# A two-layer RWKV stack with an FP4 feed-forward: where the recurrence keeps its scaled factors, how GpSimd's sums are cut, and what the planner reckons between engines

## The chip, the core and the metric

The kernel runs on one core of one Trainium2 chip. The metric is the device time of one execution in microseconds (us). Before the change the median of three runs is 3125.28 us (3124.25 to 3128.61). All of the arithmetic is float32.

The engines are named as the profile names them: PE (TensorE; PEld is its loading of weights), DVE (VectorE), ACT (ScalarE), POOL (GpSimd) and SP (SyncE, which here only issues DMAs).

## What is computed

The input `x` has 2 batches of 4096 rows of 256 channels. A conditioning vector gives six rows per batch (`sa, ca, ga, sb, cb, gb`). Cut to what matters, the reference is:

```python
h = layernorm(x) * (1 + ca) + sa
for i in range(2):                          # two RWKV layers
    h = h + time_mix(ln(h) * ln1_w[i])
    h = h + channel_mix(ln(h) * ln2_w[i])
x = x + ga * (ln(h) * ln_out_w)
h = layernorm(x) * (1 + cb) + sb
return x + gb * fp4_ffn(h)                  # gate, up, silu, down; inputs and weights rounded to FP4

# time_mix: sx = shift(x) - x; five inputs x + sx * (maa + mix), where mix comes of a small
# tanh projection; from them r = sigmoid(.. Wr), k = .. Wk, v = .. Wv, g = silu(.. Wg),
# w = exp(-exp(time_decay + tanh(.. td_w1) @ td_w2)); then, for each head of 64 channels:
def step(state, rt, kt, vt, wt):
    kv = kt[:, None] * vt[None, :]
    out = rt @ (state + u[:, None] * kv)
    return state * wt[:, None] + kv, out
# the outputs are normalised by head, times gn_w plus gn_b, times g, times Wo
# channel_mix: sigmoid(.. cWr) * (square(relu(.. cWk)) @ cWv)
```

## The kernel before

**Tiles and streams.** A tile is 256 rows of one batch (`TT`), so each batch has 16 tiles, and each tile passes two layers and the feed-forward. There are 64 passes of `time_mix`, of `channel_mix` and of the recurrence, and 64 feed-forward chunks of 128 rows. The work is written as generators, called streams: `first_layer` and `second_layer` for each batch, `ffn_inputs`, two `ffn_chunks`, `ffn_weights` and `conditioning`. A pass alone has long waits for one engine by another. Several streams run side by side so that one fills the waits of the others.

**The planner.** No order of instructions is written by hand. `Plan.record` takes each operation into a queue of its stream, with a reckoned duration (`weight`). `Plan.run` then gives the operations out one by one: of those that could start soonest it takes the one with the least lateness and age (`min(can)`). When an operation may start is reckoned in `Plan.after`: the end of its producer plus `LAT` of the producer's engine plus `SEEN` of the consumer's (55 ns for PE, 80 for POOL, 35 for others), or plus `SAME` if both are on one engine. A change of the form of PE's tiles is charged `TURN` (94 ns), and leaving ACT's table 1283 ns. The whole plan is drawn `PLANS` = 8 times with different random ages (`JITTER`), and the drawing whose reckoned end is earliest is built. Each engine then executes its own list in order; semaphores hold an instruction until its operands are there. The planner's numbers thus set only the order.

**Buffers.** Work lives in a stock of 36 equal buffers (`SLOTS`, called `slot` in the profile), 4 double ones for r and k of the recurrence (`SLOTS2`, `slot2_n` in the code, `slot` in the profile), 5 `long` ones for the feed-forward, and 5 PSUM banks (`bank`). A stream is only read further while at least `LEAST` buffers are free.

**The recurrence, `wkv`.** It is computed in chunks of 128 rows, without a step for each row. For levels l = 0 to 6, blocks of 2^l rows meet their neighbours: `products(l)` forms the scores between the two halves of each pair of blocks, and then one DVE operation multiplies half of the elements of r and k in place by the decay of the neighbouring block (the half that `pair_view` picks: r in the later half of each pair, k in the earlier). The products of level l need the factors after the updates 0 to l-1. Level 0 uses copies of r and k with the bonus u in them (`r0`, `k0`, two slots). In the code before, the products are issued at these steps of the loop:

```python
for m in {0: (), 1: (0, 1)}.get(l, (l,)):
    products(m)
```

so levels 0 and 1 come together and each later level alone. Scores of levels 0 to 3 and of levels 4 to 6 lie in the same PSUM columns (`pa`). They are copied from there at l = 3 (by DVE under a mask, into `diag`) and at l = 6 (level 4 by DVE, 5 and 6 by ACT into `attn`). Then follow transposes of k, the state's products and the output's. The whole is under `head_lock`: one pass at a time.

**PE's forms.** Most matmuls use the array whole, 128 rows by 128 columns. The products of levels 0 to 5 use pieces of 64 rows by 32 columns (32 matmuls for each level 0 to 4, 16 for level 5), level 6 pieces of 64 by 64 (8), and the small projections pieces of 32 by 128, 64 by 128 and 128 by 64. The profile writes the form ahead of the shape (`64*32`), and counts each float32 matmul twice.

**The five inputs, `to_input`.** For each of the two channel blocks j, a DVE operation forms (mix + maa) * sx for 256 rows out of a PSUM bank; then one POOL operation adds x to both blocks (128 x 512). There are 5 in each of 64 passes, thus 320.

Every recorded operation stands in one line of the profile, L294 (line 294, where `give_out` calls it), so groups are told apart by the names of tiles and by shape. The functions that the diff touches follow.

Of the kernel before, what the change touches and what calls it, by code (L numbers as in the profile page):

```python
# [10 lines left out]
F32 = mybir.dt.float32  # L11
# [3 lines left out]
ALU = mybir.AluOpType  # L15
# [3 lines left out]
P = 128  # L19
D = 256  # L20
J = D // P
TT = 256
# [15 lines left out]
TURNS = 30.0  # L38
SLOTS = 36
STAGGER = (12, 60)  # L40
PLANS, JITTER = 8, 8.0
SLOTS2 = 4
TINY = 16
LONG = 5
AHEAD_OPS = 24
# [72 lines left out]
class Plan:  # L118
# [10 lines left out]

    LAT = {"tensor": 170.0, "vector": 0.0, "scalar": 0.0, "gpsimd": 0.0, "sync": 2600.0, "load": 0.0}  # L130


    LAP = {"vector": 84.0, "scalar": 100.0, "gpsimd": 40.0}
    SEEN = {"tensor": 55.0, "gpsimd": 80.0}
    SAME = {"vector": 34.0, "scalar": 25.0, "gpsimd": 80.0}

# [323 lines left out]
def rwkv_adaln_fp4_kernel(ctx: ExitStack, tc: tile.TileContext, a: dict, out: bass.AP):  # L460
# [77 lines left out]
    def take_slot():  # L538
        return pl.take(stock)
# [4 lines left out]
    def give(*ts):  # L544
        stock.extend(ts)
# [7 lines left out]
    def v4(t):  # L553
        return t[:, : J * TT].rearrange("p (c j t) -> p c j t", c=C, j=J)
# [113 lines left out]
    for i in range(L):  # L668
        for b in range(B):
            nc.gpsimd.memset(state[i][b], 0.0)  # L670
            for m in range(2):
                nc.gpsimd.memset(carry[i][b][m], 0.0)
    diag = keep.tile([P, 2, C, J, 32], F32, name="diag")
    attn = keep.tile([P, 2, C, J, P], F32, name="attn")
# [83 lines left out]
    def shifted(h, ln_w, car):  # L758

        xn_s = take_slot()  # L760
        xn = v3(xn_s)
        yield from layernorm(h, xn)
        bk, pt = to_channels(xn)
        x_s = take_slot()
        xT = x_s.rearrange("p (j t) -> p j t", j=J)
        pl.vector.tensor_copy(xT[:, :, 0:1], car)
        for j in range(J):
            pl.scalar.activation(xT[:, j, 1:], pt[:, j, :], AF.Copy, scale=ln_w[:, j : j + 1])
        pl.close(bk)
        give(xn_s)  # L770
        pl.vector.tensor_copy(car, xT[:, :, TT : TT + 1])
        sx_s = take_slot()
        sx = v3(sx_s)
        pl.gpsimd.tensor_tensor(sx, xT[:, :, 0:TT], xT[:, :, 1:], ALU.subtract)
        yield
        return xT[:, :, 1:], sx, x_s, sx_s

    def lerp(x, sx, maa):
        m_s = take_slot()
        m = v3(m_s)  # L780
        for j in range(J):
            pl.vector.scalar_tensor_tensor(
                m[:, j, :], sx[:, j, :], maa[:, j : j + 1], x[:, j, :], ALU.mult, ALU.add
            )
        return m, m_s
# [18 lines left out]

    def pair_view(rk, h, n):

        v = rk[:, h : h + 1]
        return bass.AP(v.tensor, v.offset, [v.ap[0], [J * TT - h, 2], [2 * h, n], [1, h]])

# [27 lines left out]
    def wkv(i, b, rk_s, dec_s, v_s):  # L837

        S = state[i][b]
        rk = rk_s[:, : 2 * J * TT]  # L840
        r, k = (rk[:, m * J * TT : (m + 1) * J * TT].rearrange(
            "p (c j t) -> p c j t", c=C, j=J) for m in range(2))
        dec, v = v4(dec_s), v3(v_s)
        yield from take(head_lock, (i, b))
        late = pl.cur.late
        pl.cur.late = late - RUSH
        r0_s, k0_s = take_slot(), take_slot()
        r0, k0 = v4(r0_s), v4(k0_s)
        with_bonus(r0, r, 0, lay[i]["time_first"])
# [6 lines left out]
        tots_s = take_slot()  # L856
        at = 0
        def products(l):
            R, K = (r0, k0) if l == 0 else (r, k)
            wid = 64 if l == 6 else 32  # L860
            pv = pa[:, :, level_cols(l)].rearrange("p a (c j t) -> p a c j t", c=C, j=J)

            if l < NLEV:
                at0 = [(q, q) for q in (0, 32, 64, 96)]
            else:
                at0 = [(0, 32), (64, 96)] if l == 5 else [(0, 64)]
            for c in range(C):
                for j in range(J):
                    for s0, t0 in at0:
                        for p in range(2):  # L870
                            hp = slice(p * HS, (p + 1) * HS)
                            mm(
                                pv[s0 : s0 + wid, p, c, j, :], K[hp, c, j, s0 : s0 + wid],
                                queries(R[hp, c, j, t0 : t0 + wid], l), True, True,
                            )

        for l in range(7):
            h = 1 << l

            for m in {0: (), 1: (0, 1)}.get(l, (l,)):  # L880
                products(m)
            if l == 1:
                give(r0_s, k0_s)

# [3 lines left out]
            tv = tot.rearrange("p (n two) -> p n two", two=2)  # L888
            upd = pair_view(rk, h, n)
            pl.vector.tensor_tensor(  # L890
                upd, upd, tv.rearrange("p n m -> p m n").unsqueeze(3).to_broadcast([P, 2, n, h]), ALU.mult
            )
# [21 lines left out]
            yield  # L914
        give(dec_s)
        tot = tot.rearrange("p (c j) -> p c j", c=C)
        for q in range(4):
# [60 lines left out]
    def time_mix(i, b, h):  # L978
# [7 lines left out]
        for k in range(J):  # L986
            mm(pm[:, TT : 2 * TT], w["w1"][:, k, P:], xx[:, k, :], k == 0, k == J - 1)
        give(xx_s)
        mix_s = take_slot()
        mixa, mixb = mix_s[:, :TT], mix_s[:, TT : 2 * TT]  # L990
# [3 lines left out]

        def to_input(o, maa):

            m_s = take_slot()
            m = v3(m_s)
            for j in range(J):
                pl.vector.scalar_tensor_tensor(  # L1000
                    m[:, j, :], o[j], maa[:, j : j + 1], sx[:, j, :], ALU.add, ALU.mult
                )
            pl.gpsimd.tensor_tensor(m, m, x, ALU.add)
            return m_s

        def branch_pair(f, g, maa_f, maa_g):

            bks, os = zip(*(pl.bank() for _ in range(2)))
            for j in range(J):
                for e, o in zip((f, g), os):  # L1010
                    mm(
                        o[:, j * TT : (j + 1) * TT], w["w2"][e][:, j * P : (j + 1) * P],
                        mixa[E * e : E * (e + 1), :], True, True,
                    )
            ms = []
            for bk, o, maa in zip(bks, os, (maa_f, maa_g)):
                ms.append(to_input([o[:, j * TT : (j + 1) * TT] for j in range(J)], maa))
                pl.close(bk)
            return ms
# [11 lines left out]
        bk, pg = proj(w["Wg"], v3(xg_s))  # L1031
        give(xg_s)
        g_s = take_slot()
        g_t = v3(g_s)
# [6 lines left out]
        for k in range(J):  # L1041
            for c in range(C):
# [3 lines left out]
                )  # L1046
        give(xw_s)
        td_s = take_slot()
        td = td_s[:, :P]
        pl.scalar.activation(td, pd[:, :P], AF.Tanh)  # L1050
        pl.close(bk)
        yield
        xk_s, xv_s = branch_pair(1, 2, w["k_maa"], w["v_maa"])
        give(mix_s, x_s, sx_s)
        rk_s = take_slot2()
# [31 lines left out]
        if not w["centred"]:  # L1087
# [8 lines left out]
            )  # L1096
        v_s = take_slot()
        xv = v3(xv_s)
        bk, o = proj_tok(w["Wv"], [xv[:, k, :] for k in range(J)])
        pl.scalar.copy(v3(v_s), o)  # L1100
        pl.close(bk)
        give(xv_s)
        yield

        o_s = yield from wkv(i, b, rk_s, dec_s, v_s)
        bk, pt = to_channels(v3(o_s))
        give(o_s)
        oT_s = take_slot()
        oT = v3(oT_s)
# [15 lines left out]
    def channel_mix(i, b, h):  # L1125
        w = lay[i]
        x, sx, x_s, sx_s = yield from shifted(h, w["ln2_w"], carry[i][b][1])
        xk, xk_s = lerp(x, sx, w["ck_maa"])
        xr, xr_s = lerp(x, sx, w["cr_maa"])
        give(x_s, sx_s)  # L1130
        yield
        kks = []
        for g in range(FD // P // 2):
            bk, o = pl.bank()
            o = halves(o)
            for m in range(2):
                n0 = (2 * g + m) * P
                for k in range(J):
                    mm(o[:, m, :], w["cWk"][:, k, n0 : n0 + P], xk[:, k, :], k == 0, k == J - 1)
            kks.append(take_slot())  # L1140
            kg = v3(kks[-1])
            pl.scalar.activation(kg, o, AF.Relu)
            pl.close(bk)
            pl.scalar.activation(kg, kg, AF.Square)
            yield
        give(xk_s)
        sr_s = take_slot()
        sr = v3(sr_s)
        bk, o = proj_tok(w["cWr"], [xr[:, k, :] for k in range(J)])
        pl.scalar.activation(sr, o, AF.Sigmoid)  # L1150
        pl.close(bk)
        give(xr_s)
        yield
# [152 lines left out]
    def ffn_inputs():  # L1306
# [3 lines left out]
        for n in range(B * NT):  # L1310
# [5 lines left out]
            xn = v3(xn_s)  # L1316
            yield from layernorm_rows(x1, xn, rows["cb"][b], lambda c: rows["sb"][b])
            p_s = pl.take(long)
            yield from fp4(pl, xn_s, C * D, P, scales[0], p_s)
            long.append(p_s)  # L1320
            xq_s = take_slot()
            xqT = v3(xq_s)
            bk, pt = to_channels(xn)
            pl.scalar.copy(xqT, pt)
            pl.close(bk)
            give(xn_s)
            left = []
# [14 lines left out]
    def ffn_chunk(c, b, t, x1_s, xq_s, left):  # L1342
        HF = FI // 2
        cs_ = slice(c * P, (c + 1) * P)
        x1, xqT = v3(x1_s), v3(xq_s)
        hb_s = pl.take(long)
        hb = hb_s[:, :FI]
        for s in range(2):
# [12 lines left out]
            pl.close(bk)  # L1361
            yield
        p_s = pl.take(long)
        yield from fp4(pl, hb_s, FI, P, scales[1 + c], p_s)
        long.append(p_s)
        hT_s = pl.take(long)
        hT = hT_s.rearrange("p (f n) -> p f n", f=NF)
        for g in range(2):
# [8 lines left out]
            yield  # L1377
        long.append(hb_s)
        bk, y = pl.bank()
# [90 lines left out]
```

## Time and profile before

| | |
|---|---|
| median of three runs | 3125.28 us |
| the profiled execution | 3123.61 us |
| its span, first to last instruction | 3121.7 us |
| mean granted PE clock | 0.981 |
| instructions | 89,338 |
| PE's records: matmuls of form 64*32 into `pa` | 22,528 |
| ACT's loads of a table | 127, 1283 ns each |
| POOL's sums of two slots, 128 x 512, and 128 x 256 | 384 and 64 |

The span is the time between the first and the last instruction; 1.9 us of the profiled execution lie outside it. A group's line gives its busy time, the mean duration of one instruction in ns, and after the bar the idle time of the engine ahead of it, with what ended that idle time. Busy time of PE is not time at its full speed, since a matmul that starts late, or follows another form, still counts as busy from its start to a modelled end. The step from one start to the next is the better measure there.

### The profile page before, as it was taken

How to read it: one execution, taken by the hardware profiler on the slowest of the kernel's cores; microseconds unless marked ns; L12 is line 12 of the kernel's file. 1: busy time of each engine (PE TensorE's matmuls, PEld its weight loads, DVE VectorE, ACT ScalarE, POOL GpSimd, SP SyncE). 2: the span in 40 equal slices, each digit the busy share in tenths (PEclk: the TensorE clock that was granted, in tenths of full speed). 3: DMA queues.
4: the chain of work that ended last, by engine and by line, in shares of the span. 5: the costliest groups of instructions: out<-in, count | busy, mean ns of one | idle time of the engine just before them, and what ended most of it. 6: DMA issues, size and time to landing. Idle time of an engine off the chain costs nothing. (4 is left out here: it accounts for less than half of the span.)

```text
span 3121.7 us, 89338 instructions
## 1 busy us (share of the span) xinstructions
PE 2984.9 (96%) x38460; PEld 2412.9 (77%) x38460; DVE 2365.4 (76%) x6146; ACT 1615.4 (52%) x3362; POOL 940.6 (30%) x888
## 2 busy tenths in 40 slices
PE   6899999999999999999999999999999999999997
PEld 4777778778787777877778787787878778787775
DVE  6785778777877777778777787777777778766877
ACT  3565555545555556455454655546445455455442
POOL 2233323223233332332323233232332323331220
PEclk9899999999999999999999999999999999999989
DMA  4000000000000000000000000000000000000000
GB/s 141 20 14 5 10 7 15 7 15 7 9 12 7 16 8 11 11 6 17 5 11 11 5 18 5 14 8 9 13 6 17 5 8 15 9 9 9 8 13 11
DMA packets 35725, 42.53 MB, mean 14 GB/s; under 512 B 2817, under 2 KB 33537, under 8 KB 35329
## 3 DMA queue, kind: packets, MB, share of 16 engines
q1 hardware_dynamic: 35328, 36.81, 3.7%
q8 instruction: 302, 4.95, 0.7%
q14 instruction: 95, 0.77, 0.1%
HBM read 28.41 MB, written 8.39 MB: 12 GB/s over the span
## 5 line engine op out<-in xcount | busy, mean ns | idle before, releaser
L294 POOL TENSOR_TENSOR slot<-slot,slot 128x512 f32<-128x512 f32 (+1 forms) x448 | 508.9, 1152 | 961.5 <-DVE slot L294 682.0
L294 ACT ACTIVATE slot<-bank 128x512 f32<-128x512 f32 (+2 forms) x644 | 331.6, 519 | 682.8 <-PE bank L294 661.1
L294 POOL TENSOR_TENSOR tiny<-tiny,nhalf 128x2 f32<-128x2 f32 (+1 forms) x288 | 289.3, 1009 | 869.6 <-DVE tiny L294 789.4
L294 DVE TENSOR_TENSOR slot<-slot,slot 128x512 f32<-128x512 f32 x512 | 372.1, 728 | 110.2 <-PE pa L294 79.6
L294 PE MATMUL bank<-slot,small 32*128 32x256 f32 (+3 forms) x2816 | 393.3, 361 | 8.9 <-DVE slot L294 4.4
L294 PE MATMUL bank<-slot,cWk 128*128 128x256 f32 x1536 | 367.9, 385 | 2.5 <-DVE slot L294 2.0
L294 PE MATMUL bank<-cWv,slot 128*128 128x256 f32 x1536 | 343.8, 380 | 0.0
L294 PEld LDWEIGHTS pa<-slot 64*32 64x32 f32 x19456 | 224.0, 109 | 154.2 <-DVE diag L294 54.2
L294 PEld LDWEIGHTS bank<-slot,small 32*128 32x128 f32 (+3 forms) x2816 | 272.3, 178 | 88.3 <-issue 33.8
L294 PEld LDWEIGHTS bank<-slot,cWk 128*128 128x128 f32 x1536 | 284.5, 191 | 46.9 <-DVE slot L294 4.3
L294 PEld LDWEIGHTS bank<-cWv,slot 128*128 128x128 f32 x1536 | 289.2, 190 | 39.8 <-issue 0.3
L294 PE MATMUL pa<-slot 64*32 64x16 f32 x19456 | 266.2, 191 | 43.0 <-DVE diag L294 23.7
L294 ACT ACTIVATE slot<-bank,small 128x256 f32<-128x256 f32 (+1 forms) x640 | 248.4, 449 | 111.6 <-PE bank L294 109.9
L294 DVE SCALAR_TENSOR_TENSOR slot<-bank,small,slot 128x256 f32<-128x256 f32 x640 | 271.8, 473 | 24.9 <-PE bank L294 23.9
L294 DVE TENSOR_TENSOR slot<-slot,bank 128x512 f32<-128x512 f32 x192 | 131.0, 682 | 189.3 <-PE bank L294 143.0
L294 POOL TENSOR_TENSOR slot<-slot 128x512 f32<-128x512 f32 x128 | 141.9, 1111 | 346.8 <-ACT slot L294 272.3
L294 ACT ACTIVATE slot<-slot 128x512 f32<-128x512 f32 x288 | 181.3, 633 | 42.8 <-DVE slot L294 38.0
L294 DVE TENSOR_TENSOR long<-long,bank 128x352 f32<-128x352 f32 x256 | 131.1, 514 | 93.0 <-ACT long L294 69.8
L294 DVE SCALAR_TENSOR_TENSOR slot<-slot,small,slot 128x256 f32<-128x256 f32 x384 | 186.7, 518 | 16.8 <-POOL slot L294 16.7
L294 PE MATMUL bank<-ident,slot 128*128 128x128 f32 x1152 | 178.0, 283 | 14.0 <-ACT slot L294 8.6
L294 ACT COPY slot<-bank 128x512 f32<-128x512 f32 x224 | 130.3, 586 | 111.3 <-PE bank L294 107.3
L294 PE MATMUL bank<-wd,long 128*128 128x256 f32 x768 | 184.7, 391 | 1.2 <-ACT long L294 1.2
(106 smaller groups left out, 5362.5 us busy)
## 6 DMA issues: line engine op xcount, KB each, us to landing
slot<-in_L_attn_x_dram SPq DMA_DIRECT2D x64, 256.0 KB, 2.7
out_dram<-slot SPq DMA_DIRECT2D x64, 128.0 KB, 1.7
slot<-in_L_wmod_dram SPq DMA_DIRECT2D x6, 256.0 KB, 7.7
cWk<-in_L_attn_cWk_dram SPq DMA_DIRECT2D x2, 768.0 KB, 8.2
cWv<-in_L_attn_cWv_dram SPq DMA_DIRECT2D x2, 768.0 KB, 9.4
small<-in_small_dram SPq DMA_DIRECT2D x2, 718.0 KB, 8.3
long<-in_L_ffn_w_down_dram SPq DMA_DIRECT2D x2, 352.0 KB, 2.8
long<-in_L_ffn_w_gate_dram SPq DMA_DIRECT2D x5, 128.0 KB, 7.2
```

The source lines that it names most:

```text
L294: fn(*[real(v) for v in a], **{n: real(v) for n, v in k.items()})
```

## The change

It has five parts.

1. **GpSimd's sums.** `to_input` adds x by channel block, in two POOL operations of 128 x 256 in place of one of 128 x 512.
2. **The planner's numbers.** `LAT` becomes 120 ns for DVE, 60 for ACT and 200 for POOL (each was 0); `SAME` for DVE becomes 84 (was 34). `PLANS` becomes 1: the first drawing is built.
3. **A second place for the recurrence's factors.** A tile `rk2` of the size of r and k together is kept for the whole kernel. It takes the place of `r0` and `k0`, and after level 0 it is the second place between which the updates move: update 2 reads `rk` and writes `rk2`, update 4 goes back, the others are in place (`place`). When the place changes, ACT copies the half that the update leaves alone. The products of levels 2 and 3 are issued together, and those of 4 and 5.
4. **Results in operands' buffers.** Twelve results are written over an operand whose last reader they are: the shifted x, the tanh mix, g, the decay's hidden part, the input of v, v, the normalised output, in `channel_mix` one input, the last squared part and the sigmoid, in the feed-forward the transposed input and the transposed hidden part. 
5. **Stocks.** 37 slots, 3 double buffers, 4 long ones; streams wait where a double or a long buffer is taken and none is free.

The diff, cut to its core:

```diff
-SLOTS = 36
+SLOTS = 37
-PLANS, JITTER = 8, 8.0
-SLOTS2 = 4
+PLANS, JITTER = 1, 8.0
+SLOTS2 = 3
-LONG = 5
+LONG = 4
...
-    LAT = {"tensor": 170.0, "vector": 0.0, "scalar": 0.0, "gpsimd": 0.0, "sync": 2600.0, "load": 0.0}
+    LAT = {"tensor": 170.0, "vector": 120.0, "scalar": 60.0, "gpsimd": 200.0, "sync": 2600.0, "load": 0.0}
...
-    SAME = {"vector": 34.0, "scalar": 25.0, "gpsimd": 80.0}
+    SAME = {"vector": 84.0, "scalar": 25.0, "gpsimd": 80.0}
...
+    rk2 = keep.tile([P, 2 * J * TT], F32, name="rk2")
...
 def shifted(h, ln_w, car):
-        x_s = take_slot()
+        x_s = xn_s
...
+    def parts(rk):
+        return (
+            rk[:, m * J * TT : (m + 1) * J * TT].rearrange("p (c j t) -> p c j t", c=C, j=J) for m in range(2)
+        )
-    def pair_view(rk, h, n):
-        v = rk[:, h : h + 1]
-        return bass.AP(v.tensor, v.offset, [v.ap[0], [J * TT - h, 2], [2 * h, n], [1, h]])
+    def pair_view(rk, h, n, changed=True):
+        v = rk[:, h : h + 1] if changed else rk[:, :1]
+        return bass.AP(
+            v.tensor, v.offset, [v.ap[0], [J * TT - h if changed else J * TT + h, 2], [2 * h, n], [1, h]]
+        )
...
 def wkv(i, b, rk_s, dec_s, v_s):
-        r0_s, k0_s = take_slot(), take_slot()
-        r0, k0 = v4(r0_s), v4(k0_s)
+        r0, k0 = parts(rk2)
+        r, k = parts(rk)
...
+        place = {0: rk2, 1: rk, 2: rk, 3: rk2, 4: rk2, 5: rk, 6: rk, 7: rk}
         def products(l):
-            R, K = (r0, k0) if l == 0 else (r, k)
+            R, K = parts(place[l])
...
-            for m in {0: (), 1: (0, 1)}.get(l, (l,)):
+            for m in {1: (0, 1), 3: (2, 3), 5: (4, 5), 6: (6,)}.get(l, ()):
                 products(m)
-            if l == 1:
-                give(r0_s, k0_s)
...
-            upd = pair_view(rk, h, n)
+            here, there = place[l] if l else rk, place[l + 1]
+            if here is not there:
+                pl.scalar.copy(pair_view(there, h, n, False), pair_view(here, h, n, False))
             pl.vector.tensor_tensor(
-                upd, upd, tv.rearrange("p n m -> p m n").unsqueeze(3).to_broadcast([P, 2, n, h]), ALU.mult
+                pair_view(there, h, n), pair_view(here, h, n), tv.rearrange("p n m -> p m n").unsqueeze(3).to_broadcast([P, 2, n, h]), ALU.mult
             )
...
 def time_mix(i, b, h):
-        give(xx_s)
-        mix_s = take_slot()
+        mix_s = xx_s
...
-            pl.gpsimd.tensor_tensor(m, m, x, ALU.add)
+            for j in range(J):
+                pl.gpsimd.tensor_tensor(m[:, j, :], m[:, j, :], x[:, j, :], ALU.add)
...
-        xk_s, xv_s = branch_pair(1, 2, w["k_maa"], w["v_maa"])
-        give(mix_s, x_s, sx_s)
+        xk_s, xv_s = branch_pair(1, 2, w["k_maa"], w["v_maa"], sx_s)
+        give(mix_s, x_s)
+        while not stock2:
+            yield
         rk_s = take_slot2()
...
 def ffn_chunk(c, b, t, x1_s, xq_s, left):
+        while not long:
+            yield
         hb_s = pl.take(long)
...
+        while not long:
+            yield
         p_s = pl.take(long)
...
-        hT_s = pl.take(long)
+        hT_s = hb_s
```

More of the change, by code (lines that the diff above doesn't have):

```diff
@@ L769, in shifted @@
         pl.close(bk)
-        give(xn_s)
         pl.vector.tensor_copy(car, xT[:, :, TT : TT + 1])
@@ L776, in shifted, with lerp @@
         return xT[:, :, 1:], sx, x_s, sx_s
-    def lerp(x, sx, maa):
-        m_s = take_slot()
+    def lerp(x, sx, maa, m_s=None):
+        m_s = m_s or take_slot()
         m = v3(m_s)
@@ L840, in wkv @@
         rk = rk_s[:, : 2 * J * TT]
-        r, k = (rk[:, m * J * TT : (m + 1) * J * TT].rearrange(
-            "p (c j t) -> p c j t", c=C, j=J) for m in range(2))
         dec, v = v4(dec_s), v3(v_s)
@@ L915, in wkv @@
         give(dec_s)
+        r, k = parts(rk)
         tot = tot.rearrange("p (c j) -> p c j", c=C)
@@ L993, in time_mix, with to_input @@
         yield
-        def to_input(o, maa):
-            m_s = take_slot()
+        def to_input(o, maa, m_s=None):
+            m_s = m_s or take_slot()
             m = v3(m_s)
@@ L1002, in to_input, with branch_pair @@
                 )
-            pl.gpsimd.tensor_tensor(m, m, x, ALU.add)
+            for j in range(J):
+                pl.gpsimd.tensor_tensor(m[:, j, :], m[:, j, :], x[:, j, :], ALU.add)
             return m_s
-        def branch_pair(f, g, maa_f, maa_g):
+        def branch_pair(f, g, maa_f, maa_g, m_s=None):
             bks, os = zip(*(pl.bank() for _ in range(2)))
@@ L1015, in branch_pair @@
             ms = []
-            for bk, o, maa in zip(bks, os, (maa_f, maa_g)):
-                ms.append(to_input([o[:, j * TT : (j + 1) * TT] for j in range(J)], maa))
+            for bk, o, maa, s in zip(bks, os, (maa_f, maa_g), (None, m_s)):
+                ms.append(to_input([o[:, j * TT : (j + 1) * TT] for j in range(J)], maa, s))
                 pl.close(bk)
@@ L1031, in time_mix @@
         bk, pg = proj(w["Wg"], v3(xg_s))
-        give(xg_s)
-        g_s = take_slot()
+        g_s = xg_s
         g_t = v3(g_s)
@@ L1046, in time_mix @@
                 )
-        give(xw_s)
-        td_s = take_slot()
+        td_s = xw_s
         td = td_s[:, :P]
@@ L1096, in time_mix @@
             )
-        v_s = take_slot()
+        v_s = xv_s
         xv = v3(xv_s)
@@ L1101, in time_mix @@
         pl.close(bk)
-        give(xv_s)
         yield
@@ L1106, in time_mix @@
         bk, pt = to_channels(v3(o_s))
-        give(o_s)
-        oT_s = take_slot()
+        oT_s = o_s
         oT = v3(oT_s)
@@ L1128, in channel_mix @@
         xk, xk_s = lerp(x, sx, w["ck_maa"])
-        xr, xr_s = lerp(x, sx, w["cr_maa"])
-        give(x_s, sx_s)
+        xr, xr_s = lerp(x, sx, w["cr_maa"], sx_s)
+        give(x_s)
         yield
@@ L1139, in channel_mix @@
                     mm(o[:, m, :], w["cWk"][:, k, n0 : n0 + P], xk[:, k, :], k == 0, k == J - 1)
-            kks.append(take_slot())
+            kks.append(take_slot() if g < FD // P // 2 - 1 else xk_s)
             kg = v3(kks[-1])
@@ L1145, in channel_mix @@
             yield
-        give(xk_s)
-        sr_s = take_slot()
+        sr_s = xr_s
         sr = v3(sr_s)
@@ L1151, in channel_mix @@
         pl.close(bk)
-        give(xr_s)
         yield
@@ L1320, in ffn_inputs @@
             long.append(p_s)
-            xq_s = take_slot()
+            xq_s = xn_s
             xqT = v3(xq_s)
@@ L1325, in ffn_inputs @@
             pl.close(bk)
-            give(xn_s)
             left = []
@@ L1362, in ffn_chunk @@
             yield
+        while not long:
+            yield
         p_s = pl.take(long)
@@ L1377, in ffn_chunk @@
             yield
-        long.append(hb_s)
         bk, y = pl.bank()
```

## The prediction

> **What bounds the kernel now.** I read the page's busy shares and slices first:
>
> ```profile
> PE 2984.9 (96%) x38460; PEld 2412.9 (77%) x38460; DVE 2365.4 (76%) x6146; ACT 1615.4 (52%) x3362; POOL 940.6 (30%) x888
> ...
> PE   6899999999999999999999999999999999999997
> DVE  6785778777877777778777787777777778766877
> ```
>
> PE is busy in nine tenths or more of every slice but the first two and the last; no other engine is near. So work of DVE, ACT or POOL is free while PE need not wait for it. A busy PE is not one at full speed, so I read the timeline of PE alone, start to start (columns: start, duration, engine, line, operation):
>
> ```profile
> 1508.79 1.35 PE L294 MATMUL bank<-wu,slot 128*128 128x352 f32 x4
> 1509.98 1.35 PE L294 MATMUL bank<-wg,slot 128*128 128x352 f32 x4
> ...
> 1549.94 1.35 PE L294 MATMUL bank<-wu,slot 128*128 128x352 f32 x4
> 1551.21 0.73 PE L294 MATMUL pa<-slot 64*32 64x16 f32 x64
> 1551.87 1.99 PE L294 MATMUL bank<-slot,small 128*128 128x256 f32 x8
> ...
> 1577.97 0.72 PE L294 MATMUL pa<-slot,slot 64*32 64x32 f32 x62
> ...
> 1579.18 1.13 PE L294 MATMUL bank<-slot,small 32*128 32x256 f32 x8
> ```
>
> Four matmuls with `wu` take 1.19 us when the same form follows (1508.79 to 1509.98), and 1.27 when products of the recurrence follow (1549.94 to 1551.21). Products of one level take 0.66 (1551.21 to 1551.87), but two levels in a row 1.21 (1577.97 to 1579.18), not 1.32. **Each change of form costs about 0.1 us.** Over all records the same subtraction gives 0.094 us for leaving the whole array (0.309 after a 128x256 matmul, 0.216 otherwise). The order has 1228 such changes, so about 120 us.
>
> The same reading gives PE's waits: every step less the undisturbed step of its kind and successor sums to 239 us. 50 us of it lie before 234 us, 19 in the last 80, 170 between. By size, 108 us are waits under 0.25 us each. About 33 us stand before products of the recurrence.
>
> **The change, part by part**, against the profiled execution (3123.61 us, span 3121.7; the median of the runs is 1.7 above it). Counts after the change come from the built order of instructions.
>
> *Second place: forms of PE.* The same 20,016 matmuls are issued, but levels 2 with 3 and 4 with 5 stand together. Runs of form 64*32 fall from 310 to 187, and all changes of form from 1228 to 981. 247 x 0.10 = **-25 us**; the other way, 123 runs fewer at 0.11 + 0.09 = 0.20 us is also 25. PE sets the end, so this counts in full, unless waits take its place.
>
> *Second place: waits.* A level must wait for the update before it, one DVE operation of 0.73:
>
> ```profile
> L294 DVE TENSOR_TENSOR slot<-slot,slot 128x512 f32<-128x512 f32 x512 | 372.1, 728 | 110.2 <-PE pa L294 79.6 <-ACT slot L294 27.7
> L294 DVE COPY_PREDICATED diag<-masks,pa 128x128 f32<-128x128 int32 x256 | 83.1, 325 | 19.6 <-PE pa L294 18.3
> L294 ACT COPY slot<-bank 128x512 f32<-128x512 f32 x224 | 130.3, 586 | 111.3 <-PE bank L294 107.3
> ```
>
> With the ways there and back (0.04 and 0.055, the usual ends of waits in the trace) a gap between levels needs 0.82 us of other PE work; between 3 and 4 it needs 1.46, since a product of decays (0.20) and the masked copy of level 0 (0.435) must also be done, which clears the PSUM columns. Afterwards there are three gaps: before level 2 two updates, the product between them and the way to the second, 1.9; before level 4 two updates, the product and the copy, 2.2; before level 6, 0.82. The order tells what PE has there, priced by the rows: before, a median of 1.9 us in every gap; after, 2.8, 2.8 and 1.4. Summing the shortfalls over the 64 passes gives 20 us before (42 gaps too short) and 28 after (35 gaps): **+8 us**. The 128 ACT copies (586 ns is the nearest row, 75 us in all) run beside the second update, which is longer, so they cost nothing on PE if ACT is free. If an ACT operation stands ahead, the products behind wait for it, and all of PE's list behind them.
>
> *Larger reckoned ways.* No instruction changes, only the order. The old numbers equal what the trace shows at the end of waits (55 ns DVE to PE), so the old plan sets a consumer to the very instant and any drift becomes a wait. The new ones put it 60 to 200 ns later if other work is ready. That can remove waits of that size, the 108 us, at most; at least nothing. I take a third, **-35 us**, nearer to nothing, because drift of the plan against the chip can be larger than the margin. On DVE after DVE the trace has 0.10 between end and start, which 84 ns meets better than 34; this is part of the third.
>
> *One drawing in place of eight.* What the best of eight is worth on the chip is in no row. The drawings differ only in the order of operations of nearly equal age. As an estimate, it moves at most a sixteenth of the 170 us of waits in the middle, 10 us either way. I take **+5**.
>
> *GpSimd's halves.*
>
> ```profile
> L294 POOL TENSOR_TENSOR slot<-slot,slot 128x512 f32<-128x512 f32 x384 | 454.8, 1201 | 801.5 <-DVE slot L294 529.9 <-ACT slot L294 184.0 <-issue 36.0
> ...
> L294 POOL TENSOR_TENSOR slot<-slot,slot 128x256 f32<-128x256 f32 x64 | 54.6, 853 | 160.0 <-DVE slot L294 152.1 <-DVE tiny L294 3.4 <-PE bank L294 3.2
> ```
>
> The half costs 0.71 of the whole, so 320 x (2 x 853 - 1201) = +162 us of POOL, to 1102 of 3100 (36%). The Trainium skill (GPSIMD Engine Reference, Elementwise — side-by-side cycle accounting) explains such an add by its elements, some 4497 ns for 2048; by that share, an estimate, a half costs half and the cut nothing. The rows are of this very operation, so I take +162, hidden by POOL's idle time. For PE nothing comes of it: the second half is ready after the second DVE operation and one sum, 2 x 0.47 + 0.85 = 1.8 us, or if the first sum is late 0.47 + 2 x 0.85 = 2.2, against 0.95 + 1.20 = 2.15. POOL's sums also hold DVE's operations with two SBUF operands (728 ns above against 686 for those with no sum beside them); a quarter more of sums adds some 10 us to DVE, which at 76% is covered. Without that cover it would be those 10 us.
>
> *ACT's tables.* The order has 111 loads, 16 fewer:
>
> ```profile
> 1531.73 1.28 ACT L294 ACT_TABLE_LOAD   x1
> 1533.03 0.37 ACT L294 ACTIVATE slot<-bank,small 128x128 f32<-128x128 f32 x1
> ```
>
> The skill (ScalarE: Activation LUTs, What ACT_TABLE_LOAD costs) adds 1380 ns of draining to each, 43 us for 16. Here the next activation starts 1.30 us after the load's start, so I count 16 x 1.283 = 21 us. ACT goes to 1615 + 75 - 21 = 1670 us, 54%: not on the path either way.
>
> *Results in operands' buffers, stocks.* Each result needs all of its operand read anyway, so no new wait is on the path. The exception is the two carried columns, which DVE now writes only after PE's transposes; 128 copies of 176 ns are queued with the DVE work behind them, and the order puts them behind it: nothing. Against that stand three double buffers and four long ones, where the tail (FP4 chains on DVE, seven tenths PE busy) may pause: between 0 and 10 us, nothing taken, since both orders end in the same two exposed chains.
>
> **Sum:** -25 + 8 - 35 + 5 = -47 us on 3125.3: **3078 us**.
>
> **Rivals.** *The margins buy nothing (0.17):* -25 + 8 + 5 = -12, 3113 us. For it speaks that 131 of the 239 us are waits over 0.25 us. Against: the many small ones.
>
> *The margins buy more (0.12):* two thirds of the 108 us, -72, and no loss in the recurrence: -25 - 72 + 5 = -92, 3033 us. For: with fewer buffers taken the streams reach further. Against: the pass has only three double buffers.
>
> *Slower: the recurrence waits on two updates and ACT (0.15).* Before levels 2 and 4 PE now depends on a chain of 1.9 to 2.2 us and on an ACT copy in an in-order queue; if ACT stands in a table load (1.28) or two activations, PE stops. If each of the 128 gaps lost 0.5 us more than I count, that is +64 us; with the margins a wash (0) and the drawing +5, -25 + 8 + 64 + 5 = +52, 3177 us. It decides from (25 - 8 - 5) / 128 = 0.09 us for each gap if the margins buy nothing, from 0.37 us if they buy the 35. Against: by the order only 30 of these 128 gaps are too short, and ACT is idle 46% of the time.
>
> *A poor drawing, or streams held by three double buffers (0.04)*: the margins buy nothing, the drawing costs its 10, the tail its 10, and 15 us of waits come back with fewer passes to fill them (an estimate, a tenth of the 170): -25 + 8 + 10 + 10 + 15 = +18, 3143 us.
>
> **How the numbers follow.** Forecast 0.52. About 0.2% (6 us) is what a measurement of this kernel can tell from no change. Faster: 0.52 + 0.12 + 0.11 of the 0.17 at 3113 = 0.75. Same: the other 0.06 of that case. Slower: 0.15 + 0.04 = 0.19. The range runs from 3035, nearly the good rival, to 3140, short of the far end of the slow one.
>
> **What would show it.** Right: changes of form near 981 and PE's step before products unchanged; PE's busy time down by some 20 us or more, its idle time of 137 us (span less busy) down as well; short waits before `bank<-ident` and `bank<-S` gone. The sums at 128x256 should stay near 0.8 us and POOL near 1100. Wrong: PE waiting before `pa` for ACT or DVE by 60 us or more, ACT's new copies much above 0.6 us, a longer tail, or a lower granted clock than 0.981.

## The result, and the profile after

The changed kernel takes 3149.8 us in the median of four runs (3146.72 to 3156.59), beside 3125.01 for the kernel before: a ratio of 1.0077 with a 95% interval of 1.0058 to 1.0096. By the ratio it is slower by 24 us, where 47 us less had been forecast. The profiled execution has a span of 3144.7 us, 23 more than before.

The page of the changed kernel: busy shares, two rows of slices, and the granted clock of PE in tenths.

```profile
PE 2967.7 (94%) x38460; PEld 2425.8 (77%) x38460; DVE 2358.7 (75%) x6146; ACT 1658.5 (53%) x3474; POOL 1017.3 (32%) x1208
...
PE   6899999999999999999999999999999998999987
...
PEclk8899999999999999999999999999999998999998
```

The granted clock before:

```profile
PEclk9899999999999999999999999999999999999989
```

PE's busy time fell by 17 us, and the span rose by 23, so PE is idle for 177 us and not 137. No other engine has become the bound. The mean granted clock is 0.975 after 0.981.

The timeline of PE, around the recurrence (start, duration, engine, line, operation, and in brackets the idle time before and what ended it):

```profile
1499.64 0.72 PE L294 MATMUL pa<-rk 64*32 64x32 f32 x62
...
1500.84 2.86 PE L294 MATMUL bank<-wd,long 128*128 128x256 f32 x12
1503.63 0.73 PE L294 MATMUL pa<-slot 64*32 64x16 f32 x64
1505.23 0.73 PE L294 MATMUL pa<-rk 64*32 64x16 f32 x64 [0.87 <-DVE rk L294]
...
1569.49 1.45 PE L294 MATMUL bank<-wg,slot 128*128 128x352 f32 x4
1570.78 1.35 PE L294 MATMUL bank<-wu,slot 128*128 128x352 f32 x4
1573.48 0.70 PE L294 MATMUL pa<-slot 64*32 64x16 f32 x62 [1.35 <-DVE diag L294]
```

Two joined levels take 1.20 us (1499.64 to 1500.84), as before. The order on PE has 981 changes of form, as counted. But level 3 at 1505.23, next to level 2 in PE's order, waits 0.87 us for the moved update. Levels 2 and 3 at 1573.48 wait 1.35 us for a masked copy of DVE, in spite of the matmuls with `wg` and `wu` ahead of them.

Four groups that the change made or altered:

```profile
L294 POOL TENSOR_TENSOR slot<-slot,slot 128x256 f32<-128x256 f32 x704 | 494.3, 730 | 569.5 <-DVE slot L294 546.3 <-DVE tiny L294 21.7 <-POOL slot L294 0.3
...
L294 ACT ACT_TABLE_LOAD x111 | 142.4, 1283 | 27.4 <-PE bank L294 15.3 <-DVE masks L517 7.1 <-DVE slot L294 3.3
...
L294 ACT COPY rk<-slot 128x512 f32<-128x512 f32 x64 | 39.7, 620 | 84.3 <-DVE slot L294 68.7 <-DVE rk L294 7.9 <-PE bank L294 7.7
L294 ACT COPY slot<-rk 128x512 f32<-128x512 f32 x64 | 39.5, 617 | 103.6 <-DVE rk L294 102.1 <-DVE tiny L294 1.2
```

The new ACT copies take 0.62 us each (the two last lines). ACT is idle ahead of them for 188 us in all, nearly always waiting for DVE.

**An account of the span.** The subtraction used in the forecast (each step on PE less the undisturbed step) can be made for any trace. The span is then the changes of form at 0.097 us (between the forecast's 0.094 and 0.1), plus the waits, plus a rest. "Waits" are all delays of PE in excess of the undisturbed step, those at a lowered clock among them. The rest is the undisturbed steps, and so nearly the same wherever the same matmuls are issued.

| profiled execution | changes of form | at 0.097 | waits | rest | span |
|---|---|---|---|---|---|
| before | 1228 | 119 | 258 | 2744 | 3121.7 |
| changed | 981 | 95 | 312 | 2738 | 3144.7 |

So the forms gave 24 us and the rest 6, and waits took 54. The question is where these waits come from.

### The profile page after: what moved, and what is told of

It reads as the page before. It is cut to its first block, busy times and chain, and to the rows that moved or that the text cites. A ratio compares the mean times of both kernels' runs of the same rounds, so it can differ in the third digit from the quotient of the medians.

```text
span 3144.7 us, 90004 instructions
## 1 busy us (share of the span) xinstructions
PE 2967.7 (94%) x38460; PEld 2425.8 (77%) x38460; DVE 2358.7 (75%) x6146; ACT 1658.5 (53%) x3474; POOL 1017.3 (32%) x1208
## 4 chain that ended last, share of the span: by engine, by line
PE 44%; DVE 9%; ACT 6%; issue 1%; POOL 0%; POOLq 0%; ACTq 0%; DVEq 0%
PE bank L294 40%; DVE slot L294 4%; PE pa L294 3%; ACT slot L294 2%; ACT attn L294 2%; DVE long L294 2%; ACT rk L294 2%; ACT L294 1%; DVE tiny L294 1%; DVE scales L294 1%; DVE rk L294 1%; PE kv L294 1%; DVE diag L294 1%; ACT long L294 0%; DVE S L294 0%
## 5 line engine op out<-in xcount | busy, mean ns | idle before, releaser
L294 POOL TENSOR_TENSOR slot<-slot,slot 128x256 f32<-128x256 f32 (+1 forms) x768 | 581.2, 783 | 742.6 <-DVE slot L294 546.3
L294 PE MATMUL bank<-slot,small 32*128 32x256 f32 (+3 forms) x2816 | 385.9, 359 | 10.4 <-DVE slot L294 5.7
L294 PE MATMUL bank<-slot,cWk 128*128 128x256 f32 x1536 | 361.5, 385 | 5.9 <-DVE slot L294 5.7
L294 DVE TENSOR_TENSOR slot<-slot,slot 128x512 f32<-128x512 f32 x320 | 231.4, 724 | 89.0 <-PE pa L294 48.3
L294 PE MATMUL pa<-slot 64*32 64x16 f32 x11264 | 172.9, 194 | 38.5 <-DVE diag L294 16.4
L294 PEld LDWEIGHTS pa<-slot 64*32 64x32 f32 x11264 | 144.8, 110 | 81.7 <-DVE diag L294 29.9
L294 PEld LDWEIGHTS bank<-ident,slot 128*128 128x128 f32 x1152 | 138.1, 144 | 65.8 <-DVE slot L294 22.8
```

Source lines behind the costliest of these rows:

```text
L294: fn(*[real(v) for v in a], **{n: real(v) for n, v in k.items()})
```

## The experiments

Every result is a ratio to the kernel before, run on the same chip. Drawings are named by the seed of the planner's random ages, from 0. "Best of eight" is the drawing with the earliest end by the planner's own reckoning. Three theories of the added waits stood against each other: D, the drawing makes them; R, the new recurrence makes them, whatever the drawing; M, the larger ways between engines (the margins) send the planner to worse orders.

### The drawing, or the recurrence, or the ways

Changed kernel with eight drawings (`after_p8`), and its second drawing alone (`after_s1`):

```diff
-PLANS, JITTER = 1, 8.0
+PLANS, JITTER = 8, 8.0
```
```diff
-    best = min(range(PLANS), key=lambda seed: plan(seed, True))
+    best = 1
```

> The changed kernel with the best of eight drawings. Theory D: 3115 to 3130, at or below the kernel before. Theories R and M: within 8 us of the changed kernel (3142 to 3158).

> The changed kernel with its second drawing (random seed 1), nothing else. It shows how far two drawings of one code lie apart. Theory D: 10 us or more from 3150, on either side. Theories R and M: within 8 us of it.

Measured: 3097.98 us, ratio 0.9895 (0.9874 to 0.9916), and 3152.37 us, 1.0061 (1.0037 to 1.0086). One number in the planner makes of a kernel that is 0.8% slower one that is 1% faster, faster still than theory D expected. The second drawing lies within 8 us of the first, as theories R and M expected and D did not; the further drawings below show that not all lie so close.

Kernel before with one drawing (`before_p1`, `PLANS` = 1):

> The kernel before with its first drawing in place of the best of eight. If the drawing carries the loss (theory D), this is slower than before by 15 to 30 us (3140 to 3155), with 40 us more of waits on PE and more time at half clock. If the recurrence's new gaps carry it (theory R) or the margins do (theory M), it is within 8 us of before (3117 to 3133).

Measured: ratio 0.9996 (0.9986 to 1.0007). This run turned out to tell nothing of the drawings: its instructions stand in the same order on every engine as those of the kernel before. The old best of eight is its first drawing. It shows only how well one program repeats. To see other drawings of the old code, three were run by themselves:

```diff
-    best = min(range(PLANS), key=lambda seed: plan(seed, True))
+    best = 1        # 2 and 3 in the others
```

> The kernel before with its second drawing (seed 1); its own best of eight turned out to be its first drawing, so the earlier run with one drawing was the same program. Theory D (one code's drawings lie some 50 us apart, and the old first one is a lucky one): 3145 to 3185. Theory R (the new recurrence is what waits longer, whatever the drawing): within 8 us of the kernel before.

> The kernel before with its third drawing (seed 2). Theory D: 3145 to 3200, above the first as well. Theory R: within 8 us of the kernel before.

> The kernel before with its fourth drawing, reckoned second of eight, well behind the first. Theory D and a reckoning that tells: 3150 to 3170. Then all the old drawings but the first lie above all the new ones of like rank.

Measured: 1.0125 (1.0109 to 1.0140), 1.0227 (1.0208 to 1.0246) and 1.0140 (1.0122 to 1.0159). The old code's other drawings are slower by 39 to 71 us than its first. Their ratios also lie above those of every drawing of the changed code that was run. So theory R falls: with the new recurrence in both, `after_p8` is 57 us faster than the changed kernel, and the old recurrence waits as long as the new when its drawing is poor.

The waits view shows it. First the kernel before, then the changed kernel, its best of eight, and the old code's third drawing (engine and tile that waited, what it waited for: total us, times, longest):

```profile
PE bank L294 <- DVE slot L294: 25.9, 19, 13.3
...
PE bank L294 <- DVE long L294: 18.5, 11, 7.4
```
```profile
PE bank L294 <- DVE slot L294: 47.7, 30, 13.6
...
PE bank L294 <- DVE long L294: 11.7, 6, 4.1
```
```profile
PE bank L294 <- DVE slot L294: 26.3, 15, 14.0
PE bank L294 <- DVE long L294: 22.6, 9, 9.0
```
```profile
PE bank L294 <- DVE slot L294: 44.2, 24, 13.8
PE bank L294 <- DVE long L294: 33.7, 12, 9.3
```

PE's waits for DVE's results go up by 15 us from the first to the second kernel, are back within 5 us of the first in the third, and are 34 us above it in the fourth, which has the old recurrence.

### Does the planner's reckoning tell the drawings apart?

Three more drawings of the changed kernel (`best = 2`, `best = 3`, `best = 28`):

> The changed kernel with its third drawing, which the planner itself reckons the latest of eight. If the planner's reckoning tells drawings apart on the chip: the slowest of the changed kernel's, 3155 to 3180. If drawings differ by chance that the planner does not see: anywhere from 3095 to 3160.

> The changed kernel with its fourth drawing, reckoned second of eight. If the reckoning tells: 3105 to 3130. If chance: about the mean of the others, 3130 to 3155.

> The changed kernel with the drawing that the planner reckons the earliest of forty. If the reckoning tells: at or below the best of eight, 3080 to 3100. If chance: 3130 to 3155.

Measured: 1.0108 (1.0090 to 1.0125), 0.9997 (0.9988 to 1.0007), 0.9973 (0.9960 to 0.9987). Put in the planner's order from the earliest end, the changed kernel's six drawings measure 0.9973 (earliest of forty), 0.9895 (best of eight), 0.9997, 1.0077 (the change as given), 1.0061, 1.0108. The old code's four measure 1.0000, 1.0140, 1.0125, 1.0227. The order is kept but for neighbours. So the reckoning tells good drawings from poor ones, with an error of up to 0.8%: the earliest of forty isn't faster than the best of eight. How much of the 0.9895 is chance isn't known. Without any choice, the first four drawings of each code average 1.0123 (old) and 1.0061 (new). That is 19 us for the change, and with four drawings each and this spread it isn't clear of chance.

The accounts of these runs:

| drawing | changes of form | waits | rest | span |
|---|---|---|---|---|
| old, 0 (the kernel before) | 1228 | 258 | 2744 | 3121.7 |
| old, 1 | 1266 | 294 | 2751 | 3167.6 |
| old, 2 | 1253 | 326 | 2747 | 3193.9 |
| old, 3 | 1255 | 304 | 2752 | 3178.3 |
| new, 0 (the changed kernel) | 981 | 312 | 2738 | 3144.7 |
| new, 1 | 998 | 322 | 2737 | 3156.2 |
| new, 2 | 1006 | 324 | 2736 | 3156.7 |
| new, 3 | 1005 | 298 | 2740 | 3135.6 |
| new, best of eight | 1020 | 263 | 2740 | 3102.0 |
| new, earliest of forty | 978 | 284 | 2741 | 3119.7 |

Within one code the rest moves by up to 8 us, as little as it must with the same matmuls, and the changes of form by 4 us, while the waits move by 61 us (new) and 68 us (old): a drawing is good or poor by its waits. Between the codes the first four drawings differ by 24.5 us in forms (1250.5 and 997.5 changes in the mean), by 11 in the rest, and the new ones wait 18 us longer (314 against 295.5). The old four have a standard deviation of 28 us in their waits, so that last difference is not shown to be anything but chance.

### The parts, each at the best of eight

The old ways between engines, in the changed code's first drawing (`after_lat`), in its best of eight (`alat_b8`), and the reverse, the new ways in the old code (`blat_b8`):

```diff
-    LAT = {"tensor": 170.0, "vector": 120.0, "scalar": 60.0, "gpsimd": 200.0, "sync": 2600.0, "load": 0.0}
+    LAT = {"tensor": 170.0, "vector": 0.0, "scalar": 0.0, "gpsimd": 0.0, "sync": 2600.0, "load": 0.0}
-    SAME = {"vector": 84.0, "scalar": 25.0, "gpsimd": 80.0}
+    SAME = {"vector": 34.0, "scalar": 25.0, "gpsimd": 80.0}
```

> The changed kernel with the old ways between engines (0, 0, 0 and 34 ns). Theory M, that the margins send the planner to worse orders: 3120 to 3130. Theory R: within 8 us of 3150. My forecast's own claim, that the margins save 35 us of waits: 3170 to 3190.

> The changed kernel with the old ways between engines (0, 0, 0, 34 ns), the best of its eight drawings. If the margins save the 35 us that the forecast gave them: 3125 to 3140, against 3098 with them. If they save nothing: 3090 to 3108. If they harm: below 3090.

> The kernel before with the new ways between engines alone, best of its eight drawings. Margins worth 35 us: 3085 to 3100. Worth nothing: between the kernel before (3125, a lucky first drawing) and 3150.

Measured: 1.0101 (1.0075 to 1.0127) beside 1.0077 for the changed kernel; 1.0019 (1.0005 to 1.0032) beside 0.9895; 1.0115 (1.0091 to 1.0140) beside 1.0000. By the first two the new ways save 7 us (within the intervals) and 39, by the third they cost 36. `after_lat` with its 3163.85 us met none of the three forecasts made for it. Each pair also compares two drawings, and one drawing is worth tens of us. Theory M finds no support, since in neither pair is the changed kernel faster with the old ways. What the ways are worth stays open.

The old recurrence in the changed kernel (`one_b8`: `r0` and `k0` in slots, updates in place, 39 slots), the second place with each level alone (`alone_b8`), and the new recurrence alone in the old code (`two_b8`, 34 slots):

```diff
-            for m in {1: (0, 1), 3: (2, 3), 5: (4, 5), 6: (6,)}.get(l, ()):
+            for m in {0: (), 1: (0, 1)}.get(l, (l,)):
```

(the diff of `alone_b8`; the two others exchange `wkv` and `pair_view` whole.)

> The changed kernel with the recurrence of before (r0 and k0 in slots, updates in place, each level alone, the room of rk2 as two more slots), the best of its eight drawings. If the fewer changes of form are worth their 25 us: 1220 or so changes again and 3115 to 3135, against 3098 for the changed kernel with the best of eight. If the second place costs as much in waits as it saves in forms: 3090 to 3105.

> The changed kernel with its second place, but the products of each level issued alone as before; best of its eight drawings. Only the joining of levels is undone. By the forms: 25 us above 3098, thus 3115 to 3135. If joining levels lengthens the waits by as much: 3090 to 3105.

> The kernel before with the second place and the joined levels alone (34 slots, to make room for rk2), best of its eight drawings. By the forms 25 us below the kernel before: 3095 to 3110. If fewer slots or the longer gaps eat it: 3120 or more.

Measured: 1.0009 (0.9996 to 1.0022), 1.0061 (1.0044 to 1.0078) and 1.0010 (0.9995 to 1.0025). Their accounts:

| kernel | changes of form | waits | rest | span |
|---|---|---|---|---|
| changed, best of eight | 1020 | 263 | 2740 | 3102.0 |
| with the old recurrence | 1185 | 281 | 2738 | 3134.3 |
| levels alone | 1078 | 298 | 2744 | 3146.5 |
| old code with the new recurrence | 1032 | 292 | 2744 | 3136.3 |

The old recurrence brings 165 changes back, 16 us, and its waits are 18 us longer. With levels issued alone only 58 changes come back. The planner often puts two levels together by itself: PE has 220 runs of the form 64*32, where the joined code has 189 and the old recurrence 311. The loss of this kernel is 35 us of waits. In the old code the new recurrence saves 196 changes, 19 us, and 34 us of waits take that back. So the saving by forms is there in each, and each time the waits weigh as much or more. With one drawing of each it is not shown whether these waits belong to the part or to the drawing.

GpSimd's sums whole again (`asum_b8`):

```diff
-            for j in range(J):
-                pl.gpsimd.tensor_tensor(m[:, j, :], m[:, j, :], x[:, j, :], ALU.add)
+            pl.gpsimd.tensor_tensor(m, m, x, ALU.add)
```

> The changed kernel with GpSimd's sums whole again (128 x 512), best of its eight drawings. If the cut is hidden, as the forecast has it: 3090 to 3108, POOL's busy time down by some 70 us (the measured halves are 0.73 us and not 0.85). If the halves help PE by feeding it earlier: 3110 to 3125. If they hold DVE up: below 3090.

Measured: 0.9940 (0.9916 to 0.9964); the profiled span is 3100.3, that of the cut sums at the best of eight 3102.0, with 267 and 263 us of waits. POOL is busy for 953 us in place of 1018. The difference in the medians, 0.45%, is within what drawings differ by. No gain or loss of the cut is shown.

## Why the prediction was wrong

**The step that failed first is "One drawing in place of eight", put at +5 with 10 us either way.** Going from the changed kernel's own best of eight to its first drawing costs 1.0077 less 0.9895, 1.8% or 57 us; against the earliest of forty (0.9973) it still costs 33. The forecast had bounded it by a sixteenth of the 170 us of waits in the middle of the run. From drawing to drawing the waits of one code move by 61 to 68 us. And the kernel before was itself a selected drawing, with the least waits of the four that were run. Comparing a chosen drawing with an unchosen one, the change gave up most of what a choice brings. That `PLANS` cost the old code nothing was chance, its first drawing being its best. The size was not quite beyond reach beforehand: `plan` in the changed kernel, which needs no chip, reckons an end of 3011.1 us for the best of eight and of 3036.5 for the first drawing, 25 us apart.

The result missed the forecast by 71 us. The mis-sized drawing makes 52 of them by the best of eight, 28 by the earliest of forty. The other 19 to 43 us lie in the remaining terms, of which the margins' -35 is the largest.

**"Larger reckoned ways", -35, rested on a wrong pool.** The 108 us of waits under 0.25 us were taken as consumers set too close to producers. The finer count used afterwards gives 106 us for them before: 96 have no releaser at all, and only 10 end with a producer within reach of such a margin. In the changed kernel the short waits are 106 again. In the traces of the three pairs above, those that end with a releaser sum to 8 to 11 us with the old margins and to 7 to 10 with the new. So as far as the profile names a releaser, the pool was some 10 us and not 108. The view of waits points the same way for PEld, PE's loading of weights (first before, then changed):

```profile
PEld bank L294 <- issue: 92.3, 279, 13.3
...
PEld bank L294 <- DVE slot L294: 27.6, 57, 3.4
```
```profile
PEld bank L294 <- issue: 98.3, 284, 13.5
PEld bank L294 <- DVE slot L294: 50.6, 70, 8.7
```

"issue" is time in which the profile shows nothing that was waited for. It hardly moved with the margins. The wait that names a producer rose, but in the best of eight, with the same margins, it is 26.1 us again (and "issue" 102.6). So this rise belongs to the drawing, and what the margins do to the longer waits is not settled by the three pairs.

**The forms, -25, were right:** 247 changes fewer at 0.097 is 24 us, and an undisturbed pair of levels still takes 1.20. At the best of eight the changed kernel is 1.05% (33 us) faster than the one before. Its profiled span is 20 us shorter: 20 by forms and 4 by the rest, less 5 us more of waits.

**Waits before the recurrence, +8, were too small here:** waits before `pa` and `kv` rise from 66 to 84 us. PE's idle time there, first before, then changed:

```profile
PE pa L294 <- DVE slot L294: 6.3, 10, 1.2
...
PE kv L294 <- ACT slot L294: 2.1, 5, 1.0
```
```profile
PE pa L294 <- DVE slot L294: 12.9, 16, 1.7
...
PE kv L294 <- ACT slot L294: 10.5, 20, 1.3
PE pa L294 <- ACT rk L294: 7.4, 10, 1.2
```

The updates and the new copy before `pa` are the mechanism that was named; the 8 us more before `kv` were not. In the best of eight the waits before both are 63 with the same recurrence, so the size belongs to the drawing. The slow rival named this place with +64 for its 128 gaps; it carries at most 18 of the 54 us, and is not the cause.

**The hidden costs stayed hidden.** ACT has 111 loads, copies of 0.62 us for the 0.586 taken, and 1658 us in all for the forecast's 1670. POOL has 1017 and not 1102, since the row with the half sums has 0.73 us and not 0.85. The forecast's row was not "of this very operation": it holds another sum, the feed-forward chunk's output plus x. One shape has several durations on POOL: 1.37 us for 128x512 where the output is multiplied by g, 1.20 in the row before that mixes these products with the sums. Why the two sums differ is not shown. With the sums whole again the time is the same within what drawings differ by.

**The rival that came nearest** was the poor drawing with its own price, 3143 us, at a chance of 0.04. Its place was right and its price made of four small terms; the drawing alone was worth 33 to 57.

**What stays open:** the sign of the margins' effect; the parts that were not tried alone, results in operands' buffers and the stocks; and how much of the 0.9895 is luck. The best version found is the changed kernel with eight drawings, 3098 us.

## What to carry to other kernels

Where a planner with random ties makes the order, a change to the code also draws a new order, and that may be worth more than the change: here up to 70 us from drawing to drawing against 24 for the forms. Compare codes by several drawings each, or by an account that separates what the code fixes (changes of form) from what the drawing decides (waits), and ask whether the kernel before is itself a selected drawing. Before pricing a wait by a margin, look at what the profile names as its releaser.

## What the runs showed of the hardware that was not expected

The granted clock of PE has only two values in these traces, 1.0 and 0.5. The stretches at 0.5 last 3.4 us or a multiple of it, but for one that the end of the span cuts off. In the kernel before there are 20 such stretches with 116 us, in the changed one 27 with 157 us, and in its second drawing 34 with 208 us. If all of it were lost at half speed, that would be 58, 79 and 104 us, which includes time in which PE waited anyway. Of the waits counted above, 77 us (before) and 93 us (changed) are on steps at half clock, so 16 of the 54 us that were added. This is the lower clock that the forecast named as a sign of being wrong.

The time at half clock does not sort the drawings. In the old code the three slower ones have 147 to 177 us of it, more than the first. But the changed code's best of eight has 142 us, and its slowest drawing, the third, has 143. What lowers the clock is not shown by these runs.
